# Four cross-attention layers on one core: 32-row score tiles, probabilities transposed on VectorE, weighted sums on 8 or 16 TensorE tiles, five weight matrices reloaded for every batch element

## The chip, the cores and the metric

The kernel runs on one core of one Trainium2 chip. The core has five engines that run side by side and meet at semaphores: TensorE (PE in the profile, with its weight loads as PEld), VectorE (DVE), ScalarE (ACT), GpSimd (POOL) and SyncE (SP, which here only issues DMAs). TensorE reads SBUF and writes PSUM, which has eight banks of 128 partitions x 512 fp32; VectorE and ScalarE read both; GpSimd works on SBUF.

The metric is the device time of one launch in microseconds, lower is better. Everything is fp32.

## The reference

`x` (16 batch elements, 100 queries, width 256) goes through four cross-attention layers against the same context of 361 keys. Layers 0 and 3 have 16 heads of 16, layers 1 and 2 have 16 heads of 64. Cut to what matters:

```python
def attend(Q, K, V, scale):            # per batch element and head
    s = Q @ K.T * scale                # 100 x 361
    return softmax(s) @ V              # 100 x 16 or 100 x 64

# layer 0: layer norms, biases, attention, then a feed-forward block
x = x + attention(ln(x), ln(ctx)) @ wo + bo
x = x + gelu(ln(x) @ w1 + b1) @ w2 + b2          # 256 -> 1024 -> 256
# layer 1: rms norm, heads of 64, no scale
x = x + attention(rms(x), ctx) @ wo              # wq, wk, wv: 256 -> 1024
# layer 2: rotary embedding on q and k, a key mask, norm at the end
x = ln(x + attention(rope(x @ Wq), rope(ctx @ Wk), ctx @ Wv, mask) @ Wo)
# layer 3: as layer 0, without the feed-forward block
x = x + attention(ln(x), ln(ctx)) @ Wo + bo
```

## The kernel before

**A list of works, ordered by a planner.** The Python program first describes the computation as some 560 works for each batch element (`plan.add`): each names the engine or engines that may do it with an assumed occupation and latency, the buffers that it reads and writes, and the buffers that it takes from a pool of slots. `Plan.order` then simulates the engines with these costs, and emits the works in the order that it finds; a copy that may run on ACT or DVE (`copied`, L706) is put on the one that its costs favour. Priorities come from the table `ORDER`: a lag between batch elements, an offset for each place in the list, and further offsets for the first and the last element. All this happens while the kernel is built; on the chip each engine runs a fixed list in order. Two batch elements are in flight, with buffers in two sets by the parity of the element (`kT0`/`kT1` and so on).

**TensorE shapes.** TensorE is used in tiles. A projection runs as four tiles of 128 rows x 32 columns (`on_columns`, L825): one call issues four matmuls, one for each strip of 32 columns of the stationary operand. The planner calls this mode `col32`. Scores run with 32 or 64 rows (`row32`, `row64`), transposes with 64 rows. `Plan.CHANGE` charges a change of mode.

**One attention layer**, class `Attention` (L904): four units of four heads.

1. `scores` (L932, matmul at L936): the stationary operand is a head's queries (100 columns), the moving one its keys, in two halves of 181 and 180. Heads of 16 sit in strips of 32 rows of which 16 are zeroed (`by_parity`, L1202). Each head fills one PSUM bank, 100 partitions x 361; five shares (`ps_sc`) limit how many banks hold scores.
2. `exponential` (L975): DVE takes the scores out of PSUM and finds the row maximum (L991; in layer 2 the mask at L985 and the maximum at L988), ACT does the exponential and its sum (L997).
3. `softmax` (L953): DVE inverts the sums of two heads (L961), POOL multiplies each head by them (L968).
4. `transposed` (L1011): TensorE transposes the probabilities, three chunks of keys by 64 and by 36 queries, 12 transposes for a pair of heads (L1032); ACT or DVE copies them to `pT` (L711, L713).
5. `weighted` (L1052): values are the stationary operand in strips of 32, `pT` the moving one with 100 columns, three chunks of keys (L830); the result is copied to `oT`.

**Around it.** `small_heads_layer` (L1151) and `large_heads_layer` (L1251) make keys (361 columns moving), values (256 or 512 columns moving, keys in chunks of 128, 128 and 105) and queries, and project out (`project_out`, `project_out_T`). `rotated` (L874) does the rotary embedding of layer 2: DVE swaps pairs (L885), POOL multiplies by the sine (L889), DVE multiplies the PSUM original by the cosine (L892), POOL adds (L897). `feed_forward` is L1339, `batch` L1373.

**Weights.** All twelve slabs of 1 MB are loaded once (`load_slab`, L522) through SP's queue in the first 45 us and stay. SP also loads the inputs of element b + 2, each element's mask, and stores its result.

Of the kernel before, what the change touches and what calls it, by code (L numbers as in the profile page):

```python
# [17 lines left out]
P = 128  # L18
# [6 lines left out]
SKP = NKC * KP  # L25
BIG = 3.0e38
SCORE_BANKS = 5
# [4 lines left out]
for _name, _w in (  # L32
# [10 lines left out]

SLABS = (
# [12 lines left out]
    "lag": 281400, "pull": 6.35, "window": 0,  # L57
    "keep": {None: 4180, "row64": 280, "row32": 710, "col64": 3610, "col32": 5250},
    "run": {None: 3260, "row64": 33260, "row32": 18740, "col64": 46890, "col32": 300},
    "batch": (-614500, -19500, 0, 0, 0, 0, 0, 0, 0, 0, 0, 0, 0, 0, 6000, -863500),  # L60
    "place": [
        100 * k for k in (
        1530, 2179, 1302, -155, -3146, -3119, -1447, -50, 2198, -4316, -4647, -2582, -7311,
        -6990, -6791, -975, -6218, -4297, -1712, -7295, -4489, -3822, -7130, -4520, -2986,
        -5107, -1814, 2539, -585, 44, -2295, -3865, -3674, -5144, -5622, -10071, -9468, -6347,
        -6509, -5109, -6468, -10008, -6583, -10112, -6656, -7056, -6274, -9553, -10961, -12648,
        -6592, -6491, -10074, -11842, -5012, -7475, -5864, -2138, -2644, -2757, -1752, -1661,
        -3175, -1806, -475, 295, -1528, -1314, -130, -2596, -3455, -3510, -486, 819, -960, -351,
        -262, -1091, -2095, 773, 352, 609, -2745, -1077, -4127, -3906, 1115, -1980, -1044, 199,
        1113, -2251, -559, -4303, 204, 507, -7028, -6650, -4569, -6483, -2121, -3493, -985,  # L70
        -4030, 928, 291, -3776, -3852, -4367, -2262, -3068, -1405, 3055, -1796, -1471, -2884,
        -3509, -3745, -408, -473, -4075, -5224, -5147, -1610, -3815, -3333, -4064, -6731, -5900,
        -7478, -6211, -2778, -3243, -2860, 346, 2670, -1934, 358, -4143, -3642, -2093, -2165,
        -529, 13, -685, -1077, -415, 5064, -896, -533, -6410, 8, -1286, 795, -1181, 3287, 2325,
        1250, 437, 2327, 2459, -1757, -1578, -5694, -990, 2513, 7808, 7794, 4228, 183, 3326,
        3721, 2104, 3855, 1016, 3932, -5255, -932, -801, -1656, 458, -71, 3547, -2879, -7942,
        1183, -679, -3284, -3147, -4837, -4906, -3658, -1029, -5460, -1795, -2290, -3716, -633,
        -1243, 250, 3042, 115, 3644, 209, 517, 802, 3561, 2033, 8348, 2938, -2370, -768, 91,
        -3053, -3682, 21, -551, -703, 11, -1354, -76, -6811, -5354, -5457, -3261, -4456, -5041,
        -4118, -7857, -5743, -9610, -9289, -7014, -6103, -6155, -5974, -3208, -5827, -5655,  # L80
        -3748, -6019, 1222, -6204, 1169, 1555, 804, 4287, 847, 1540, 2681, 4086, 3349, 8301,
        3405, 2300, 1930, -158, 2379, 3910, 4211, 3253, -272, -266, -2428, -1347, 2024, 88,
        -3112, -7985, -3868, 994, 1277, -1300, -464, -390, 2333, 3472, 2811, 3971, 4406, 6487,
        7550, 8667, 4711, 4737, 1877, 3779, 2319, 8022, 4465, 4476, 4993, 5707, 6778, 4543,
        5848, 4450, 5898, 5280, 5713, 2599, 4430, 8324, 4133, 8528, 6706, 596, 2298, -498, -905,
        1966, -4295, -1105, -3795, -5564, -1315, 1532, -3363, -2789, -552, 18, -3105, -6266,
        -10045, 1320, -6270, -4428, -689, -4740, -3580, 963, -5363, -2314, 1942, 5363, 3756,
        3169, 735, -4085, 2025, 1750, 1971, 2138, 2974, 3519, 5203, 5507, -452, 3042, -190, 412,
        -928, -229, 3162, -526, 895, -1352, -1376, -3942, -3984, -379, -7134, -2812, 551, -6423,
        -2341, -2152, -3333, 1507, -1188, 1764, 4650, 1708, -78, 1087, 3668, 2857, -1320, -858,  # L90
        -553, -1310, -4001, -416, -2796, -2804, -3944, -3808, -3234, -2595, -5780, -8117, -7507,
        -10136, -9612, -9238, -7690, -3249, -4884, -5928, -7611, -6301, -4692, -3495, -11110,
        -9091, -6761, -5493, -6295, -1317, -740, 731, -2244, -69, -536, 1225, -1389, -3686,
        -3052, 1470, -6939, -3363, -3396, -8455, -10700, -13129, -12689, -11245, -7208, -10167,
        -10536, -5830, -7870, -7456, -6041, -4659, -7272, -4839, -3132, -1617, -5559, -2862,
        1514, 625, -188, 1018, -3554, -7159, -3278, -5544, -4708, -2643, -3131, -6058, -6394,
        1652, -6383, 298, -1138, -636, 2469, 408, -1417, 3200, 3186, 3478, 1178, 3587, 3199,
        6766, 4361, -6638, -2795, -3377, -7601, -7151, -544, 106, 696, 3907, 4138, 174, -2346,
        -2919, -5554, -4166, -6125, -7266, -5804, -4121, -1761, -2439, -2442, -6500, -2289,
# [93 lines left out]
        ),  # L193
    },
}

class Buf:
# [209 lines left out]
def tile_xattn_layers(  # L409
# [56 lines left out]
    for t in slots["prob"]:  # L466
        nc.gpsimd.memset(t[:S, SK:], 0.0)
# [1030 lines left out]
```

## Time and profile before

| what | value |
|---|---|
| runs of the kernel before | median 1938.1 us of 3 (1937.89 to 1939.73) |
| the profiled execution, first to last instruction | span 1935.2 us; no other time of this execution is given |
| granted TensorE clock, mean over the span | 0.993 |
| largest TensorE groups, busy: values of the large heads, keys of the large heads, scores, transposes (64 columns) | 367.0, 346.0, 303.3, 240.8 us |
| exponential on ACT, with its read of the sum | 602.0 + 194.0 us in 1024 pairs |
| multiplication by the inverse sum on POOL | 566.2 us in 1024 instructions |
| DMA | 29.94 MB in all, of it 5.64 MB of instructions in 344 packets |

How to read it: a group's busy time is the union of its instructions' durations. TensorE's matmuls are pipelined, so that the durations of neighbours overlap: a matmul with 100 columns has a mean duration of 250 ns, and yet dozens of them start in a microsecond. What TensorE can do in a given time is therefore read from starts, not from durations or from its busy share. The "idle before" of a group is the idle time of its engine just before its instructions, and names who ended it.

### The profile page before, as it was taken

The numbers are of one execution on the slowest core, as the hardware profiler recorded it, in microseconds if no ns is written. First come the engines' busy times: TensorE is split into PE (matmuls) and PEld (weight loads), VectorE is DVE, ScalarE is ACT, GpSimd is POOL, SyncE is SP. The second block draws the span as 40 slices with busy tenths as digits, with TensorE's granted clock in tenths as the row PEclk, the third lists the DMA queues.
The fourth block names the chain that finished last, engine by engine and source line by source line (L and its number), as shares of the span: only waits on it lengthen the run. The fifth ranks groups of instructions, "written<-read, shape, count | busy, mean of one in ns | idle before, by whom it ended". The sixth has DMA issues, their size and how long they took to land.

```text
span 1935.2 us, 99776 instructions
## 1 busy us (share of the span) xinstructions
PE 1914.6 (99%) x43881; PEld 1268.0 (66%) x43881; DVE 1294.5 (67%) x4502; ACT 1170.2 (60%) x3418; POOL 1045.9 (54%) x1682
## 2 busy tenths in 40 slices
PE   8999999999999999999999999999999999999997
PEld 4667666575766757667575675766657576575766
DVE  5556676766667666666666676667676667765776
ACT  4646556575665746657566565665657566575645
POOL 5355465555556555555645555556555555654564
PEclk9999999999999999999999999999999999999997
DMA  7000000000000000000000000000000000000000
GB/s 305 3 3 14 5 12 8 3 14 5 12 8 3 14 5 12 8 3 15 5 14 6 11 9 3 14 5 12 8 3 14 6 12 8 3 15 5 3 3 7
DMA packets 14730, 29.94 MB, mean 15 GB/s; under 512 B 3362, under 2 KB 12376, under 8 KB 12888
## 3 DMA queue, kind: packets, MB, share of 16 engines
q1 hardware_dynamic: 14296, 23.56, 3.8%
q8 instruction: 344, 5.64, 1.2%
q14 instruction: 90, 0.74, 0.1%
HBM read 21.92 MB, written 1.64 MB: 12 GB/s over the span
## 4 chain that ended last, share of the span: by engine, by line
PE 97%; DVE 1%; POOL 1%; ACT 0%; issue 0%; DMA 0%; SPq 0%; POOLq 0%; DVEq 0%; ACTq 0%
PE ps L830 70%; PE ps L936 14%; PE ps L1032 11%; PE ps L771 1%; PE ps L858 1%; PE ps L813 0%; ACT prob L997 0%; DMA slab<-slabs_dram 0%; DVE prob L991 0%; PE ps L616 0%; PE ps L665 0%; POOL prob L968 0%; DVE pT L713 0%; DVE prob L985 0%; POOL kT L897 0%
## 5 line engine op out<-in xcount | busy, mean ns | idle before, releaser
L968 POOL TENSOR_SCALAR prob<-prob,two 100x361 f32<-100x361 f32 x1024 | 566.2, 571 | 551.6 <-DVE two L961 335.2
L997 ACT ACTIVATE prob<-prob,two 100x361 f32<-100x361 f32 x1024 | 602.0, 592 | 138.6 <-DVE prob L991 87.2
L991 DVE TENSOR_SCALAR_CACHE_REDUCE prob<-ps 100x361 f32<-100x361 f32 x768 | 372.3, 530 | 143.7 <-PE ps L936 126.7
L830 PE MATMUL ps<-slab,cT 128*32 128x512 f32 (+1 forms) x3072 | 367.0, 595 | 0.0
L830 PE MATMUL ps<-cT,slab 128*32 128x361 f32 x4096 | 346.0, 468 | 0.0
L936 PE MATMUL ps<-kT,qT 32*100 32x181 f32 (+3 forms) x4096 | 303.3, 328 | 2.9 <-DVE qT L1204 1.4
L711 ACT COPY pT<-ps 128x384 f32<-128x384 f32 (+1 forms) x521 | 231.1, 492 | 93.4 <-PE ps L1032 77.4
L936 PEld LDWEIGHTS ps<-kT,qT 32*100 32x100 f32 (+1 forms) x4096 | 228.1, 164 | 74.8 <-issue 30.8
L1032 PEld LDWEIGHTS ps<-ident,prob 36*128 36x128 f32 (+1 forms) x6144 | 215.3, 140 | 85.1 <-POOL prob L968 62.8
L1032 PE MATMUL ps<-ident,prob 64*128 64x64 f32 (+1 forms) x6144 | 240.8, 227 | 1.5 <-ACT pT L711 0.8
L713 DVE COPY pT<-ps 128x384 f32<-128x384 f32 (+1 forms) x247 | 137.4, 573 | 130.9 <-PE ps L1032 128.7
L711 ACT COPY v<-ps 128x512 f32<-128x512 f32 (+1 forms) x119 | 69.7, 586 | 245.6 <-PE ps L830 161.8
L830 PEld LDWEIGHTS ps<-cT,slab 128*32 128x32 f32 x4096 | 123.1, 109 | 134.7 <-issue 122.4
L997 ACT ACTIVATION_READ_ACCUMULATOR prob<-prob,two 100x1 f32 x1024 | 194.0, 189 | 0.0
L889 POOL TENSOR_TENSOR sw<-sw,rot 128x361 f32<-128x361 f32 x128 | 105.3, 824 | 135.6 <-DVE sw L885 110.2
L830 PEld LDWEIGHTS ps<-slab,cT 128*32 128x32 f32 (+1 forms) x3072 | 85.3, 107 | 139.2 <-issue 127.3
L985 DVE TENSOR_TENSOR prob<-ps,cap 100x361 f32<-100x361 f32 x256 | 125.5, 527 | 62.6 <-PE ps L936 37.9
L830 PE MATMUL ps<-pT,v 128*32 128x100 f32 (+1 forms) x6144 | 155.3, 250 | 0.3 <-ACT pT L711 0.3
L830 PEld LDWEIGHTS ps<-pT,v 128*32 128x32 f32 (+1 forms) x6144 | 136.0, 110 | 22.7 <-issue 13.2
L897 POOL TENSOR_TENSOR kT<-kT,sw 128x361 f32<-128x361 f32 x128 | 122.5, 959 | 5.7
L988 DVE TENSOR_REDUCE two<-prob 100x1 f32<-100x361 f32 x256 | 125.6, 517 | 0.0
L830 PE MATMUL ps<-xT,slab 128*32 128x100 f32 x5120 | 124.1, 252 | 1.1 <-ACT xT L791 1.1
(105 smaller groups left out, 2329.6 us busy)
## 6 DMA issues: line engine op xcount, KB each, us to landing
slab<-slabs_dram SPq DMA_DIRECT2D x11, 1024.0 KB
ctxr<-ctx_dram SPq DMA_DIRECT2D x16, 256.0 KB
ctxr<-ctx_dram SPq DMA_DIRECT2D x16, 105.0 KB
x<-x_dram SPq DMA_DIRECT2D x16, 100.0 KB
out_dram<-x SPq DMA_DIRECT2D x16, 100.0 KB
slab<-slabs_dram SPq DMA_DIRECT2D x2, 512.0 KB
mask<-mask_dram SPq DMA_DIRECT2D x16, 45.1 KB
rows<-rowvecs_dram SPq DMA_DIRECT2D x1, 640.0 KB
```

What stands on the lines that cost most here:

```text
L711: nc.scalar.copy(dst(), src())
L713: nc.vector.tensor_copy(dst(), src())
L830: nc.tensor.matmul(out_f(at + t, at + t1), lhsT=lhsT[:, t:t1], rhs=rhs, start=start, stop=stop, tile_position=(0, at + t),)
L889: nc.gpsimd.tensor_tensor(a, a, wide(sin()), ALU.mult)
L897: nc.gpsimd.tensor_tensor(dst_f(dst.ap), dst_f(dst.ap), sw.ap[:, :n], ALU.add)
L936: nc.tensor.matmul(banks[h].ap[:S, k0:k1], lhsT=self.q_of(h), rhs=self.k_of(h)[:, k0:k1], start=(k0 == 0), stop=(k1 == SK), skip_group_che ...
L968: nc.gpsimd.tensor_scalar(p.ap[:S, :SK], p.ap[:S, :SK], rsum.ap[:S, j : j + 1], 1.0, ALU.mult, ALU.mult,)
L985: nc.vector.tensor_tensor(p(), bank.ap[:S, :SK], self.cap.ap[:S, :], ALU.min)
L988: nc.vector.tensor_reduce(neg_max.ap[:S, 0:1], p(), AX.X, ALU.max, negate=True)
L991: nc.vector.tensor_scalar(p(), bank.ap[:S, :SK], -1.0, None, ALU.mult, ALU.min, accum_out=neg_max.ap[:S, 0:1],)
L997: nc.scalar.activation(p(), p(), AF.Exp, bias=neg_max.ap[:S, 0:1], scale=1.0 if masked else -1.0, accum_out=sums.ap[:S, j : j + 1],)
L1032: nc.tensor.transpose(out[:, c, :], probs[h].ap[q0:q1, c * KP : (c + 1) * KP], ident[q0:q1, q0:q1],)
```

## The change

Every part of attention is cut anew; projections of queries, keys and outputs keep their form.

- **Scores.** The 100 queries are cut into four groups of 25 (`QG`, `QN`). A group's stationary operand is one head's block of 32 columns (25 of the head, 7 of what follows). Four heads lie below each other in the four 32-partition quadrants of one bank, one head per quadrant, and all 361 keys move in one matmul. Heads of 64 run on 8 tiles (64 x 32) and fill 2 banks, heads of 16 on 16 tiles (32 x 32) and fill 4. `qT` becomes flat, with zeros at its end.
- **Softmax.** The same steps on 128 partitions instead of 100; there are as many exponentials, multiplications and PSUM reads as before. Inverse sums come for 2 banks or 4 at once, the masked maximum for 2.
- **Transposes.** One `nc.vector.transpose` of 128 x 768 (blocks of 32 x 32, in place) for each two banks replaces the TensorE transposes and the copies out of PSUM. `pT` holds scores, probabilities and their transposes one after the other; `prob` and the shares are gone.
- **Weighted sums.** Keys come in 12 blocks of 32, the last with 9. One work sums half a layer of large heads (32 x 64 tiles, 8 at a time) or a whole layer of small heads (32 x 32 tiles, 16 at a time) into four banks.
- **Values** are laid out to match: for each block of 32 keys, head pairs go to the quadrants, with 128 (large heads) or 64 (small heads) columns moving instead of 512 or 256.
- **Rotary embedding.** PSUM is copied to `kT` or `qT` by ACT or DVE, and POOL multiplies by the cosine. The bias and parity of the small heads' queries (`by_parity`) may go to ACT too.
- **Weights.** Five slabs are no longer kept; each batch element loads them again into a ring of two slots, through SP, and a load may begin once a named score work has started.
- **Planner.** Modes are named by tile shape; the `ORDER` table is another one.

```diff
-SCORE_BANKS = 5
+NB = 12
+QG = 4
+QN = S // QG
+BLK = 32
+STREAMED = ("L0_xattn_w1", "L0_xattn_w2", "L1_xattn_wo", "L2_xattn_Wq", "L2_xattn_Wo")
...
-        "prob": slots_of("prob", 8, [P, SKP]),
-        "pT": slots_of("pT", 2, [P, 4, NKC, S]),
+        "v": slots_of("v", 3, [P, NB, P]),
+        "ring": slots_of("ring", 2, [P, 2048]),
...
+        slots[f"pT{p}"] = slots_of(f"pT{p}", 2, [P, QG, 2, SKP])
+        slots[f"vs{p}"] = slots_of(f"vs{p}", 1, [P, NB, 144])
+        slots[f"qT{p}"] = slots_of(f"qT{p}", 1, [P, 8 * S + BLK - QN + 1])
...
+    def stream(name, b, begun, after=()):
+        t = plan.buf("ring", f"{name}_{b}")
+        i = SLABS.index((name,))
+        def issue(_):
+            nc.sync.dma_start(out=t.ap, in_=slabs[i])
+        load = plan.add(
+            [("SP", 450.0, 6000.0)], issue, writes=[t], begun=begun
+        )
+        return t, load
...
         def times_cos(_):
-            nc.vector.tensor_tensor(
-                shaped(dst_f(dst.ap)), shaped(ps.ap[:, :n]), wide(cos()), ALU.mult
-            )
+            a = shaped(dst_f(dst.ap))
+            nc.gpsimd.tensor_tensor(a, a, wide(cos()), ALU.mult)
...
-        plan.add(on_dve(n), times_cos, reads=[ps, rot], writes=[dst])
+        copied(lambda: dst_f(dst.ap), lambda: ps.ap[:, :n], n, [ps], [dst])
+        plan.add(on_pool(2.3 * n), times_cos, reads=[dst, rot], writes=[dst])
...
+        def half(self, u, v):
+            name = f"{self.name}_{u}"
+            slots = [plan.buf(f"pT{self.p}", f"{name}_pT{k}") for k in range(self.rows)]
...
+            for g in range(QG):
+                self.group(u, g, slots, parts[g], f"{name}_{g}")
+            self.weighted(u, v, slots, [x for part in parts for x in part], name)
+        def group(self, u, g, slots, parts, name):
...
             def scores(_):
+                for j in range(4):
+                    for t in range(2 * n):
+                        m = 4 * u + j
+                        rows = slice(t * height, (t + 1) * height)
+                        keys = kb[m] if hd == 64 else kb[j // 2]
+                        at = m * S + g * QN
+                        nc.tensor.matmul(
+                            banks[t].ap[j * BLK : (j + 1) * BLK, :SK],
+                            lhsT=q.ap[rows, at : at + BLK], rhs=keys.ap[rows, :],
+                            start=True, stop=True, tile_position=(t * height, j * BLK),
+                        )
...
+                def divide(_, t=t):
+                    a = slots[t // 2].ap[:, g, t % 2, :SK]
+                    nc.gpsimd.tensor_scalar(a, a, inv.ap[:, t : t + 1], 1.0, ALU.mult, ALU.mult)
+                plan.add(on_pool(545), divide, reads=[inv, parts[t]], writes=[parts[t]])
+                if t % 2 == 0:
+                    continue
+                def transpose(_, t=t):
+                    a = slots[t // 2].ap[:, g].rearrange("p r s -> p (r s)")
+                    nc.vector.transpose(a, a)
+                both = parts[t - 1 : t + 1]
+                plan.add(on_dve(2 * SKP), transpose, reads=both, writes=both)
...
+                nc.vector.tensor_reduce(
+                    neg.ap[:, t - 1 : t + 1], slot.ap[:, g, :, :SK], AX.X, ALU.max, negate=True
+                )
...
-        def transposed(self, probs, pairs, name):
...
+        def weighted(self, u, v, slots, parts, name):
...
+            def fn(_):
+                for b in range(NB):
+                    n = keys_in(b)
+                    for j in range(4):
+                        rows = slice(j * BLK, j * BLK + n)
+                        for t in range(P // wide):
...
+                            nc.tensor.matmul(
+                                banks[j].ap[t * wide : (t + 1) * wide, :S].rearrange(
+                                    "p (g s) -> p g s", g=QG
+                                ),
+                                lhsT=lhsT,
+                                rhs=slots[t // 2].ap[rows, :, t % 2, b * BLK : b * BLK + QN],
+                                start=(b == 0), stop=(b == NB - 1),
+                                tile_position=(j * BLK, t * wide),
+                            )
...
-                    for c in range(2):
-                        on_columns(
-                            lambda t0, t1: ps.ap[t0:t1, :], cT.ap[:, c, j * KP : j * KP + n],
-                            w[wv][:, c, half * 512 : (half + 1) * 512], c == 0, c == 1,
-                        )
+                    for k in range(4):
+                        k0 = (4 * i + k) * BLK
+                        for c in range(2):
+                            for j in range(4):
+                                w0 = (4 * u + j) * P
+                                nc.tensor.matmul(
+                                    ps.ap[j * BLK : (j + 1) * BLK, k * P : (k + 1) * P],
+                                    lhsT=cT.ap[:, c, k0 : k0 + BLK], rhs=w[wv][:, c, w0 : w0 + P],
+                                    start=(c == 0), stop=(c == 1), tile_position=(0, j * BLK),
+                                )
...
+        for u in range(2):
+            for m in range(4):
+                keys(4 * u + m)
+            values(u)
+            att.half(u, vb[u])
+        gate = att.first[0, 2]
+        o_buf, _ = stream(wo, b, begun=[gate])
...
+        w1_buf, loaded = stream("L0_xattn_w1", b, begun=[gate])
+        w2_buf, _ = stream("L0_xattn_w2", b, begun=[loaded])
```

## The prediction

> **What bounds the kernel now.** I read the page from its top: busy shares, slices, the chain of work that ended last.
>
> ```profile
> PE 1914.6 (99%) x43881; PEld 1268.0 (66%) x43881; DVE 1294.5 (67%) x4502; ACT 1170.2 (60%) x3418; POOL 1045.9 (54%) x1682
> PE   8999999999999999999999999999999999999997
> PEclk9999999999999999999999999999999999999997
> ...
> PE 97%; DVE 1%; POOL 1%; ACT 0%; issue 0%; DMA 0%; SPq 0%; POOLq 0%; DVEq 0%; ACTq 0%
> PE ps L830 70%; PE ps L936 14%; PE ps L1032 11%; PE ps L771 1%; PE ps L858 1%; PE ps L813 0%; ACT prob L997 0%; DMA slab<-slabs_dram 0%; DVE prob L991 0%; PE ps L616 0%; PE ps L665 0%; POOL prob L968 0%; DVE pT L713 0%; DVE prob L985 0%; POOL kT L897 0%
> ```
>
> TensorE is the end of everything: 97% of the chain. The transposes of the probabilities (L1032) alone are 11% of the span, 213 us. Next the groups that the change touches, then a stretch of the timeline, whose starts give rates.
>
> ```profile
> L968 POOL TENSOR_SCALAR prob<-prob,two 100x361 f32<-100x361 f32 x1024 | 566.2, 571 | 551.6 <-DVE two L961 335.2
> L936 PE MATMUL ps<-kT,qT 32*100 32x181 f32 (+3 forms) x4096 | 303.3, 328 | 2.9 <-DVE qT L1204 1.4
> L711 ACT COPY pT<-ps 128x384 f32<-128x384 f32 (+1 forms) x521 | 231.1, 492 | 93.4 <-PE ps L1032 77.4
> L1032 PEld LDWEIGHTS ps<-ident,prob 36*128 36x128 f32 (+1 forms) x6144 | 215.3, 140 | 85.1 <-POOL prob L968 62.8
> L1032 PE MATMUL ps<-ident,prob 64*128 64x64 f32 (+1 forms) x6144 | 240.8, 227 | 1.5 <-ACT pT L711 0.8
> L713 DVE COPY pT<-ps 128x384 f32<-128x384 f32 (+1 forms) x247 | 137.4, 573 | 130.9 <-PE ps L1032 128.7
> L889 POOL TENSOR_TENSOR sw<-sw,rot 128x361 f32<-128x361 f32 x128 | 105.3, 824 | 135.6 <-DVE sw L885 110.2
> L830 PE MATMUL ps<-pT,v 128*32 128x100 f32 (+1 forms) x6144 | 155.3, 250 | 0.3 <-ACT pT L711 0.3
> L988 DVE TENSOR_REDUCE two<-prob 100x1 f32<-100x361 f32 x256 | 125.6, 517 | 0.0
> ```
>
> ```profile
> 1014.55 1.22 PE L830 MATMUL ps<-pT,v 128*32 128x100 f32 x48
> 1015.70 0.87 PE L936 MATMUL ps<-kT,qT 32*100 32x181 f32 x16
> 1016.50 1.06 PE L830 MATMUL ps<-slab,zT 128*32 128x256 f32 x16
> ...
> 1020.02 0.96 PE L1032 MATMUL ps<-ident,prob 64*128 64x64 f32 x24
> 1020.91 1.92 PE L830 MATMUL ps<-slab,cT 128*32 128x512 f32 x16
> ```
>
> From start to start, 24 transposes take 0.89 us and 16 score matmuls 0.80. The starts of single matmuls say more: on four column tiles they lie 7, 7, 7 ns apart, and a tile starts its next one 86 ns after the last (100 columns), 215 (256), 305 (361) or 430 (512): 2 ns plus 0.833 ns a column. Row tiles keep the same rule (181 columns: 154 ns for four, 152 for two); a pair of transposes takes 61.7. Every fp32 matmul of the code is two in the trace, a transpose one. At these rates all matmuls make 1761 us. Of 948 changes of tile shape, 125 (64-row scores to or from transposes, one shape) cost nothing, the others a median of 90 ns: 74 us. Each of 256 score visits loses about 80 ns on its first weights (20 us), and 12 us pass before the first full stretch. That leaves 68 of the 1935.2: waits, and a tail at half clock:
>
> ```profile
> 0.00:200.00 200.00, 191.22 (x4089) 125.88 (x4089) 116.68 (x421) 112.60 (x320) 97.45 (x179) 0.99 0.21 79
> 200.00:1800.00 1600.00, 1599.42 (x37048) 1054.80 (x37044) 1081.00 (x3763) 982.93 (x2873) 871.66 (x1383) 1.00 0.03 8
> 1800.00:1936.00 136.00, 123.99 (x2756) 87.31 (x2748) 96.81 (x321) 74.66 (x226) 76.79 (x121) 0.90 0.02 5
> ```
>
> (Columns: stretch, its length, busy PE, PEld, DVE, ACT, POOL, clock, DMA.) Before 1800 us TensorE is never short of work, so what leaves it leaves the time.
>
> **TensorE, part by part.**
> Transposes of probabilities: 6144 x 61.7/2 = -189.5 us.
> Scores: large heads 4096 matmuls on 8 tiles make 512 rounds of 303 = 155.1 (now 1024 pairs x 152 = 155.6); small heads 4096 on 16 tiles, 256 rounds = 77.6 (now 78.3). Together -1; first weights of 32 columns in place of 100, 384 visits at some 25 ns: 10 us for 20, -10.
> Weighted sums: large heads 12288 matmuls, 1536 rounds of 86 = 132, as now (6144 x 21.5). Small heads 12288 on 16 tiles: at 6.7 ns a start, sixteen need 107 ns, more than the 86 of the columns, so 768 x 107 = 82 for 66 now: +16 (lower bound 86, +0; upper bound is a rival).
> Values, large heads: 3072 rounds of 128 columns, 108.7 ns = 334 for 329: +5. Small heads: 1536 rounds of 64 columns for 384 of 256 columns (83 us). The trace has no 64-column matmul on four column tiles. By columns 55 ns a round, by the shortest round seen 86: 85 to 132 us. The transposes, 64 columns in 61.7, are the nearest row: 95, +12.
> Changes of shape: 24 score visits, 6 weighted sums and 9 other transposes for each element make 480 changes if most are neighbours and 1248 if none are: 43 to 112 us. I take 60 for each element, about today's 59: 86, +12.
> Instructions: 27,100 matmuls more, each with a weight load. Instruction packets of 16 KB (256 instructions) take 1.08 us and never followed each other within 3.3; a sixteen-tile sum needs three in 2.57. Bounds 0 to 32 x 0.67 = 21; its last packet alone is near the limit: +5.
> Sum -151: -189.5 - 11 + 16 + 17 + 12 + 5.
>
> [...] This trace has 7 ns between tiles. [...]
>
> **The other engines** lose their cover of idle time.
> DVE: -137 (its copies of `pT`), -72 (cosine, 128 x 440 and 32 x 475 ns between starts), -10 (128 inversions fewer at 76), -8 (128 maxima of 722 at 812 for 256 of 361 at 436), and 512 transposes of 768. No row shows one. From L988, 60 + 1.04 ns an element: 860 ns, 440 us, my value, since it too reads and writes SBUF lane by lane; lower bound half (two elements a clock), 205; upper bound two clocks an element, 1660 ns, 850. Sum 1508, of which 190 are copies that ACT may take. [...]
> ACT: 1170 - 231 + about 55 (copies for the rotary embedding) + about 20 (`oT` in 256 pieces of 100, not 128 of 200) = 1015, up to 1180 with DVE's copies.
> POOL: 1046 + 128 x 0.82 + 32 x 1.04 = 1184; 3 us more of memsets at the start, ahead of the first normalization, +0 to 3.
> So at 1805 us DVE stands at 73 to 84%, POOL at 66%, ACT at 56 to 65%: none is the bound. But a weighted sum now waits for 8 or 16 heads instead of 4. On POOL an element's ten cosine products (9 us) stand in the same queue as the multiplications by inverse sums, which DVE's transposes wait for; behind a waiting transpose stand DVE's reads of the other element's scores, and TensorE waits for their banks. The 62.8 us that weight loads idle on POOL at L1032 go to the weighted sums. The waits of 68 become 40 if TensorE meets fewer, 150 if each of DVE's bursts shows; I take 88, as DVE's share rises by a quarter.
> Weights: 80 loads of 1 MB. The stretch from 20 to 40 us moved 389 GB/s, so 2.7 us each, 0.9 us of SP's queue; all bare they cost 216. They are hidden by the rest of a softmax (eight heads keep DVE over 10 us) and by the other element's projections. A load that waits for a ring slot holds SP, and behind it inputs of two elements ahead, the mask and the store: an element (about 110 us) of slack. I take 0, and 0 for the start, where five slabs fewer compete. The query bias's choice of engine, `bq_e` and the flat layouts: 0, hidden under TensorE.
>
> 1935.2 - 150.5 + 20 (waits, 88 for 68) = a span of 1805. The median of the runs lies 2.9 above the profiled span: 1808.
>
> **Rivals.**
> Forecast, 1750 to 1850: TensorE still bounds, 0.50.
> Waits fall, since a TensorE that no longer waits twice for each probability is fed better (for it: 62.8 us of idle; against: busier DVE): waits 40, fewer changes (-40), 64 columns at 55 ns (-10): 1808 - 48 - 40 - 10 = 1710; 1690 to 1750, 0.12.
> Waits grow: DVE's bursts show (layer 2: 16 maskings, 8 maxima, 8 transposes, 10 shuffles, some 28 us, against 18 of TensorE). Waits 150 (+62), changes +26: 1896; 1850 to 1925, 0.14.
> Transposes at two clocks: DVE 1728 to 1918, over 0.97 that is 1782 to 1977, middle 1880; nothing in the trace speaks for it but that fp32 is wide; 0.07.
> Slower: tiles do not overlap beyond four. No matmul of this trace runs beside more than three others. Then the 24,576 weighted matmuls take 21.5 ns each (+314), the 8192 of the scores 76 (+390): 2510. It decides from 4.1 ns lost on each of these 32,768 (134 us). Against it: starts 7 ns apart, and row tiles keep the columns' rule. 0.12.
> No change, by chance of these: 0.03; slower by waits alone (222 us of them instead of 88): 0.02.
>
> A measurement tells some 0.2% (4 us) from no change. Faster: 0.50 + 0.12 + 0.14 + 0.06 of the fourth = 0.82; same 0.03; slower 0.15. Range 1710 to 1910, which leaves out the ends of three cases and the slower one.
>
> **What would show it.** Right: the chain still above 90% TensorE; weighted sums of small heads at about 107 ns for sixteen starts, of large heads 86 for eight; DVE transposes 860 ns apart; weight loads landing before TensorE asks. Wrong: starts of 16 tiles more than 10 ns apart, transposes near 1.7 us, chain shares of DVE above 15%, or TensorE waiting on the ring.

## The result and the profile after

The changed kernel took 2494.7 us, median of 4 runs (2487.5 to 2498.2), beside 1938.0 us of the kernel before in 4 runs on the same chip (1936.0 to 1939.7): 1.287 times as long, 95% interval 1.285 to 1.289. The forecast was 1808. It missed by 687 us and on the wrong side.

The page of the changed kernel, its busy rows, three of the slice and queue rows, the chain by engine, and the groups that the prediction priced:

```profile
span 2489.9 us, 153040 instructions
PE 2082.5 (84%) x71017; PEld 1463.3 (59%) x71017; DVE 1440.8 (58%) x4261; ACT 1098.7 (44%) x3245; POOL 1196.2 (48%) x1840
...
PE   7798878888788888888888988888888888788885
...
PEclk9799998999989998999889998889898999999996
...
q8 instruction: 555, 9.09, 1.5%
...
PE 79%; issue 15%; DVE 3%; POOL 2%; ACT 0%; DMA 0%; SPq 0%; POOLq 0%; DVEq 0%; ACTq 0%
...
L1091 DVE STREAM_TRANSPOSE pT<-pT 128x768 f32<-128x768 f32 x512 | 477.0, 957 | 28.7 <-POOL pT L1083 27.7
...
L1056 PE MATMUL ps<-kT,qT 32*32 32x361 f32 (+1 forms) x8192 | 385.2, 518 | 17.9 <-issue 7.8
...
L1163 PE MATMUL ps<-pT,vs 32*32 32x100 f32 x12288 | 199.6, 296 | 131.0 <-issue 119.5
L1163 PE MATMUL ps<-pT,v 32*64 32x100 f32 x12288 | 196.0, 263 | 102.5 <-issue 98.5
```

What to see: no engine is busy enough to be the bound by its own work. TensorE's share fell from 99% to 84%, VectorE's from 67% to 58%. The chain now has 15% "issue", where before it had 0%: time in which TensorE waited for nothing that the profile shows, no semaphore, no bank, no weights. The weighted sums (L1163) stood idle 234 us, 218 of them on "issue"; the large heads' line before (L830, `pT,v`) 0.3. The packets of instructions went from 344 to 555, as 71,017 matmuls with a weight load each need: 142,034 instructions in 555 packets, 256 to a packet. And the granted clock, at 0.993 before, is 0.914 on the mean: 429 us at half of full speed in place of 31. The packets of the kernel before, by its page:

```profile
q8 instruction: 344, 5.64, 1.2%
```

One such wait, in the chain of the changed kernel (start in us, length in us, what), and under it the DMA row of the same stretch, 1105 to 1121 us in 40 slices of 0.4 us, GB/s; nothing but packets of instructions moves in it:

```profile
1112.72 1.21 PE ps L944 x16
1113.93 2.48 PE ps L1163 x158
1116.41 1.85 issue
1118.26 0.40 PE ps L1163 x8
1118.66 1.35 PE ps L944 x16
```

```profile
GB/s 0 0 0 0 0 41 0 0 0 0 0 0 0 0 0 41 0 0 0 0 0 0 0 0 0 0 0 41 0 0 0 0 0 0 0 41 0 20 0 0
```

A weighted sum starts its matmuls at 13 to 16 ns each, gets through most of its 192 (the trace lacks a few records), and stops for 1.85 us with eight left, the last block of nine keys. A packet begins to arrive at 1115.8 us (the third 41), lands at 1116.7, and some 1.5 us later the sum goes on. The other pauses look the same: there are 265 of over 0.7 us between two starts, the median ends 1.39 us after the landing of a packet, and half of them end 1.32 to 1.48 us after one. Two packets never begin less than 3.25 us apart. A packet holds 128 pairs of weight load and matmul, so that TensorE gets a pair each 25 ns at the closest spacing, and each 27 at 3.5 us, the spacing on the mean in the fastest of the starved streams of experiment 4. A weighted sum uses one in 12 to 16.

Start to start, from the first matmul to the last, TensorE took 1926 us before and 2478.5 after. Of the 552 between them:

| where | us |
|---|---|
| pauses over 0.7 us between starts: 8 with 11 us before, 265 with 465 us after | +454 |
| starts at half clock, by group and shape, mean at half clock less mean at full, times their number: 10 us before, some 120 after | +110 |
| all else, that is, what the forecast's own terms were about (it had -131) | -12 |

### The profile page after: what moved, and what is told of

Its sections match the earlier page's. It is cut to its first block, busy times and chain, and to the rows that moved or that the text cites. A ratio compares the mean times of both kernels' runs of the same rounds, so it can differ in the third digit from the quotient of the medians.

```text
span 2489.9 us, 153040 instructions
## 1 busy us (share of the span) xinstructions
PE 2082.5 (84%) x71017; PEld 1463.3 (59%) x71017; DVE 1440.8 (58%) x4261; ACT 1098.7 (44%) x3245; POOL 1196.2 (48%) x1840
## 4 chain that ended last, share of the span: by engine, by line
PE 79%; issue 15%; DVE 3%; POOL 2%; ACT 0%; DMA 0%; SPq 0%; POOLq 0%; DVEq 0%; ACTq 0%
PE ps L944 29%; PE ps L1163 16%; PE ps L1423 15%; PE ps L1056 14%; PE ps L1336 4%; DVE pT L1112 1%; DVE pT L1091 1%; PE ps L885 1%; PE ps L972 0%; POOL ctxr L861 0%; POOL kT L1007 0%; POOL kT L1010 0%; PE ps L927 0%; POOL sw L1003 0%; POOL mv L850 0%
## 5 line engine op out<-in xcount | busy, mean ns | idle before, releaser
L1083 POOL TENSOR_SCALAR pT<-pT,four 128x361 f32<-128x361 f32 x1024 | 567.3, 576 | 719.7 <-DVE four L1076 718.1
L1136 ACT ACTIVATE pT<-pT,four 128x361 f32<-128x361 f32 x1024 | 601.1, 592 | 190.2 <-DVE pT L1112 115.5
L1091 DVE STREAM_TRANSPOSE pT<-pT 128x768 f32<-128x768 f32 x512 | 477.0, 957 | 28.7 <-POOL pT L1083 27.7
L1112 DVE TENSOR_SCALAR_CACHE_REDUCE pT<-ps 128x361 f32<-128x361 f32 x768 | 364.0, 528 | 159.0 <-PE ps L1056 158.2
L1423 PE MATMUL ps<-slab,cT 128*32 128x128 f32 x12288 | 393.3, 282 | 29.5 <-issue 28.7
L1423 PEld LDWEIGHTS ps<-slab,cT 128*32 128x32 f32 x12288 | 351.7, 114 | 84.3 <-issue 50.1
L1056 PE MATMUL ps<-kT,qT 32*32 32x361 f32 (+1 forms) x8192 | 385.2, 518 | 17.9 <-issue 7.8
L1163 PE MATMUL ps<-pT,vs 32*32 32x100 f32 x12288 | 199.6, 296 | 131.0 <-issue 119.5
L1163 PE MATMUL ps<-pT,v 32*64 32x100 f32 x12288 | 196.0, 263 | 102.5 <-issue 98.5
L1163 PEld LDWEIGHTS ps<-pT,vs 32*32 32x32 f32 x12288 | 159.3, 114 | 172.3 <-issue 141.7
L1163 PEld LDWEIGHTS ps<-pT,v 32*64 32x64 f32 x12288 | 171.3, 135 | 135.3 <-issue 122.3
L1136 ACT ACTIVATION_READ_ACCUMULATOR pT<-pT,four 128x1 f32 x1024 | 195.5, 191 | 0.0
```

What stands on the lines that cost most here:

```text
L1056: nc.tensor.matmul(banks[t].ap[j * BLK : (j + 1) * BLK, :SK], lhsT=q.ap[rows, at : at + BLK], rhs=keys.ap[rows, :], start=True, stop=True, ...
L1083: nc.gpsimd.tensor_scalar(a, a, inv.ap[:, t : t + 1], 1.0, ALU.mult, ALU.mult)
L1091: nc.vector.transpose(a, a)
L1112: nc.vector.tensor_scalar(p(), bank.ap[:, :SK], -1.0, None, ALU.mult, ALU.min, accum_out=neg.ap[:, t : t + 1],)
L1136: nc.scalar.activation(a, a, AF.Exp, bias=neg.ap[:, t : t + 1], scale=1.0 if masked else -1.0, accum_out=sums.ap[:, t : t + 1],)
L1163: nc.tensor.matmul(banks[j].ap[t * wide : (t + 1) * wide, :S].rearrange("p (g s) -> p g s", g=QG), lhsT=lhsT, rhs=slots[t // 2].ap[rows, : ...
```

## The experiments

Two theories were put against each other first. *Supply*: TensorE runs out of instructions, since 128 pairs can't be done in less time than a packet takes to follow the last, 3.25 us at the closest. *Four at a time*: the forecast's rival on the slower side, tiles that don't overlap beyond four. Its price of 2510 us was close to the result, so that it had to be tested. Each of the kernels was timed once, beside the kernel before on the same chip (1936.3 to 1938.0 us). All but the third, the fourth and the tenth start from the changed kernel.

**1. Half the columns, as many instructions.** The weighted sums with 50 columns in place of 100 (the first block keeps all, and the other half is left out):

```diff
+ m = QG if b == 0 else QG // 2
- rhs=slots[t // 2].ap[rows, :, t % 2, b * BLK : b * BLK + QN],
+ rhs=slots[t // 2].ap[rows, :m, t % 2, b * BLK : b * BLK + QN],
```

> The changed kernel, but each matmul of the weighted sums behind the first block of keys moves 50 columns instead of 100 (the sums of the last 50 queries then hold one block of 12). As many instructions, 46% less column work in them. Supply theory (TensorE waits for its instructions, some 3.4 us for each 256 of them): no gain, 2440 to 2500 us. Four-at-a-time theory (tiles beyond four don't overlap, a matmul costs a quarter of its columns' time): 22528 matmuls fall from 21.3 to 10.9 ns, -235, about 2260 us.

2495.9 us. 46% of the columns of 24,576 matmuls taken away, and nothing gained. Its chain, and a group:

```profile
PE 76%; issue 17%; DVE 4%; POOL 2%; ACT 1%; DMA 0%; SPq 0%; POOLq 0%; DVEq 0%; ACTq 0%
...
L1164 PE MATMUL ps<-pT,vs 32*32 32x50 f32 (+1 forms) x12288 | 157.2, 245 | 160.5 <-issue 148.8
```

The group's busy time fell by 42 us, and its idle time on "issue" rose by 29; the clock fell further, to 0.883. The columns don't bind; whatever comes with each instruction does.

**2. Half the instructions, as many columns.** Of each block's weighted matmuls every second one is left out, and the others have 200 columns in place of 100:

```diff
- for t in range(P // wide):
+ for t in range(b % 2, P // wide, 2):
- rhs=slots[t // 2].ap[rows, :, t % 2, b * BLK : b * BLK + QN],
+ rhs=slots[t // 2].ap[rows, :, :, b * BLK : b * BLK + QN],
```

> The changed kernel, but in the weighted sums one matmul moves the 200 columns of two heads and every second one is left out (the sums then mix the heads). Half the instructions there (12288 of 71017 matmuls fewer, each with its weight load), the same columns. Supply theory: taking each 128 pairs of weight load and matmul in program order at the larger of their own time and 3.4 us, the sum falls by 305 us; with a part of the lost clock that is 2050 to 2190 us. Four-at-a-time theory: the same columns cost the same, 2480 to 2500 us.

2108.3 us: 386 less for 12,288 pairs fewer, 31 ns a pair, with the work of the array unchanged. The packets fell to 460 and the pauses over 0.7 us from 465 to 232 us:

```profile
PE 1894.2 (90%) x58729; PEld 1310.5 (62%) x58729; DVE 1434.3 (68%) x4261; ACT 1090.8 (52%) x3245; POOL 1193.2 (57%) x1840
...
q8 instruction: 460, 7.54, 1.5%
...
PE 83%; issue 8%; DVE 5%; POOL 3%; ACT 0%; DMA 0%; SPq 0%; POOLq 0%; DVEq 0%; ACTq 0%
```

**3. The kernel before with more instructions.** Only its weighted sums are changed: each matmul of 100 columns becomes two of 50, on the same four tiles, 9,216 pairs more in all:

```diff
+ for s0 in (0, S // 2):
+     cols = slice(g * S + s0, g * S + s0 + S // 2)
...
- pTs[h][0].ap[:n, pTs[h][1], c, :], c == 0, c == NKC - 1,
+ pTs[h][0].ap[:n, pTs[h][1], c, s0 : s0 + S // 2], c == 0, c == NKC - 1,
```

> The kernel before, but each matmul of its weighted sums is split in two of 50 columns: 9216 pairs of weight load and matmul more, no more columns, the result the same. Supply theory: the sum of the larger of own time and 3.4 us over each 128 pairs rises by 102 us: 2000 to 2080 us. Four-at-a-time theory: nothing here runs on more than four tiles, 1938 to 1950 us.

2026.9 us, 89 more than before, and issue appears in the chain of a kernel that had none:

```profile
PE 95%; issue 3%; DVE 1%; POOL 1%; DMA 0%; ACT 0%; SPq 0%; POOLq 0%; DVEq 0%; ACTq 0%
```

No tile shape, no transpose and no transfer of the change is in this kernel. More instructions for the same columns bring "issue" by themselves: the pauses over 0.7 us went from 11 to 66 us.

**4. Streams by themselves.** Not the kernel: on an otherwise idle core, 2048 pairs of one shape after another, all tiles of the array in turn, with wide matmuls between the streams:

```python
for k in range(count // len(tiles)):
    for r, c in tiles:
        nc.tensor.matmul(
            banks[r // rows][c : c + wide, :n], lhsT=sta[r : r + rows, c : c + wide],
            rhs=mov[r : r + rows, :n], start=True, stop=True, tile_position=(r, c),
        )
```

> No attention, only streams of 1024 fp32 matmul calls (2048 pairs of weight load and matmul) one after the other, each behind 48 calls of 512 columns: four tiles of 128x32 with 100, 64 and 128 columns; eight of 32x64 and sixteen of 32x32 with 100; sixteen of 32x32 with 361; then 512 calls on eight of 64x32 with 361; then twelve times 48 calls on sixteen tiles with 100 columns and 48 calls with 512. Supply theory: 26 to 27 ns a pair in all of the first six, whatever their tiles and columns (128 columns need 27 by themselves), 38 on eight tiles with 361; the short bursts at the end run near 7 ns at their start. Four-at-a-time theory: 21.5, 13.8, 27.2, 21.5, 21.5, 76, 76 ns a pair.

| stream | ns a pair, all 2048 (the last: 1024) | ns a pair, first 128 |
|---|---|---|
| 4 tiles of 128x32, 100 columns | 28.6 | 21.2 |
| 4 tiles of 128x32, 64 columns | 27.5 | 14.1 |
| 4 tiles of 128x32, 128 columns | 28.0 | 27.3 |
| 8 tiles of 32x64, 100 columns | 27.6 | 12.4 |
| 16 tiles of 32x32, 100 columns | 27.1 | 11.2 |
| 16 tiles of 32x32, 361 columns | 28.2 | 23.2 |
| 8 tiles of 64x32, 361 columns | 37.7 | 36.4 |

The chain in the first stream of the table (start, length, what):

```profile
32.97 2.95 PE bank L35 x128
35.92 1.05 issue
36.97 2.95 PE bank L35 x128
39.92 0.78 issue
40.70 2.95 PE bank L35 x128
```

Here the packet can be seen as such: 128 matmuls, a pause, 128 matmuls, a pause, with 3.7 to 4.0 us from one to the next, and nothing else running on the core. Every stream whose first pairs took less than 27 ns ends at 27.1 to 28.6, on 4, 8 and 16 tiles alike; that of 64x32 tiles, with 36.4 in its first pairs, ran without a pause. The first 128 pairs, which lie ready, show what the tiles can do: 8 tiles take 12.4 ns where 4 take 21.2. A limit on how fast TensorE can start pairs would have held these back too. Tiles overlap well beyond four; the rival's mechanism is false, and its 2510 us was a coincidence. Short bursts did no harm: 96 pairs of 16 tiles between matmuls of 512 columns ran at 11.6 ns each on the mean, the first dozen 6 to 7 ns apart, with no pause.

**5. Fewer instructions elsewhere.** The values with 512, or 256 and 128, columns to a matmul, as many columns in all, 13,300 pairs fewer (the values that come out are others):

```diff
- for k in range(4):
-     k0 = (4 * i + k) * BLK
-     ... rhs=w[wv][:, c, w0 : w0 + P],
+ k0, w0 = 4 * i * BLK, 4 * u * P
+ ... rhs=w[wv][:, c, w0 : w0 + 4 * P],
```

> The changed kernel with the values' matmuls made 512, or 256 and 128, columns wide, so that some 13,300 fewer pairs of weight load and matmul are issued; the tiles of the weighted sums and of the scores stay as they are, and the values that come out are not the reference's. Supply theory (no 128 pairs can start faster than one packet of instructions arrives, some 3.4 us): 2250 to 2360 us, from the sum over packets (1974 us of TensorE against 2109 for the changed kernel, and the same 380 us behind it, with some of the stalls in the values' own gone). Rival (TensorE runs at most four tiles of a round at once in the weighted sums): these are untouched, and the values were bound by their columns, so 2470 to 2500 us.

2306.9 us, in the middle of the supply theory's range. The weighted sums, which the edit doesn't touch, gained themselves: 562 us from start to start in place of 616.

**6. Both cuts.** The second and the fifth at once, 45,417 pairs; the scores are untouched.

> Both at once: half of the weighted sums' and scores' smallest matmuls left out as in the second experiment, and the values' wide ones; some 45,000 pairs, about as many as the kernel before has. The sum is left out in part, and the output is not the reference's. Supply theory: 1830 to 1980 us, most likely 1925, with the issue share of the chain under 6%. Rival (four tiles at once): 2470 to 2500 us, since what is left of each round would take as long. A third way: the vector engines become the bound once TensorE is relieved; then the waits of TensorE on VectorE and GpSimd in the chain are above 10% and the time is over 2000.

1959.8 us: 535 of the 557 us are gone. The cuts take 25,600 pairs off, and with them the packets are 356, about as many as before the change. The chain shows who comes next:

```profile
q8 instruction: 356, 5.83, 1.2%
...
PE 78%; DVE 12%; POOL 6%; issue 4%; ACT 0%; POOLq 0%; DVEq 0%; ACTq 0%
```

Issue is at 4%, and VectorE and GpSimd, at 3% and 2% in the changed kernel, are at 12% and 6%. The third way that the expectation named, the vector engines as the next bound, is there by its share of the chain but not by its time.

**7. No reloads.** Two slabs are loaded once and stand for all five weights; the same matmuls in the same order:

```diff
  def stream(name, b, begun, after=()):
-     def issue(_):
-         nc.sync.dma_start(out=t.ap, in_=slabs[i])
...
-     [("SP", 450.0, 6000.0)], issue, writes=[t], begun=begun
+     [("SP", 450.0, 6000.0)], None, writes=[t], begun=begun
```

> The changed kernel with the five weights that are loaded again for each batch not loaded again: two slabs are loaded once and stand for all five, with the same number and order of instructions on TensorE; the values are then those of other weights. Supply theory: the transfers (80 of 1 MB) have no part in it, 2470 to 2510 us. Rival (the reloads delay the packets of instructions, which use the same DMA engines, or TensorE itself): more than 50 us faster, under 2440.

2380.2 us: 114 faster, and the supply theory as I held it, with no part for the transfers, was wrong here. The page has the same work and the same 555 packets:

```profile
PE 2052.6 (86%) x71017; PEld 1448.2 (61%) x71017; DVE 1439.1 (61%) x4261; ACT 1096.7 (46%) x3245; POOL 1196.4 (50%) x1840
...
PE 80%; issue 13%; DVE 4%; POOL 2%; ACT 0%; DMA 0%; SPq 0%; POOLq 0%; DVEq 0%; ACTq 0%
```

In the changed kernel no instruction of TensorE waited for the ring: the weights always landed in time (5.5 us on the median, 7.6 at most, of the 11 loads whose landing the trace tells). What fell is the pauses over 0.7 us, from 465 to 372 us. So the transfers cost nothing by being late themselves; most of what they cost is in longer pauses. Experiments 9 to 11 look at how.

**8. The sums spread out.** Each weighted sum is made into four pieces of three blocks, and TensorE's next works may come between them:

```diff
- def fn(_):
-     for b in range(NB):
+ def fn(_, blocks=range(NB)):
+     for b in blocks:
...
+ pieces[id(made)] = [lambda k=k: fn(None, range(k, k + 3)) for k in range(0, NB, 3)]
...
+ if held and work.engine == "PE":
+     held.pop(0)()
```

> The changed kernel with the weighted sums' matmuls issued in four pieces of three blocks each, with a piece of TensorE's next work between them, and the same matmuls in all. Supply theory: the long stretches of short matmuls are what starves; mixed with wide ones a packet lasts longer, so a gain of up to 200 us less some 50 for more changes of shape: 2300 to 2450 us. It can't fall below some 1930, since 555 packets of 3.47 us are still needed. Rival (tiles not overlapping): the same matmuls take as long wherever they stand, and the changes of shape come on top: 2490 to 2560 us.

2477.9 us, 17 less than the median of the changed kernel's runs, which lie 11 us apart: little, and outside both expectations. But the sums were hardly spread. What is left of a sum is issued at once when the next work of any engine uses one of its buffers, and in the trace most of the 32 sums of the small heads still run their 384 matmuls in one piece, and most of the 64 of the large heads are broken once, into 48 and 144. So the run does not show what spreading would bring. The supply theory's range was a guess; worked out afterwards for the order that ran, it gives none of that gain. Taking TensorE's time for each 128 pairs in their order, by the rates of the prediction, and never less than 3.36 us, an estimate from the packets' spacing (3.25 at the closest), the sum is 2094 us for the changed kernel and 2091 for this one: 368 and 369 of 555 packets are below the limit either way. Most neighbours of a weighted sum are values and projections, whose pairs need 14 to 28 ns: they have nothing to spare. And at 27.1 ns a pair, the fastest that a stream of the fourth experiment kept up, 71,017 pairs would take 1925 us in any order, about the time of the kernel before.

**9. Both cuts and no reloads.** The sixth and the seventh together.

> The sixth experiment (half of the smallest matmuls left out, wide values; 1959.8 us) without the five weights' reloads, as in the seventh, which took 114 us off the changed kernel. It computes the values of other weights and leaves out part of the sums. If the reloads cost by delaying packets of instructions, they cost less where TensorE seldom runs out of instructions: 1910 to 1945 us. If they cost in another way, about as much as in the changed kernel whatever TensorE runs: 1840 to 1860 us.

1924.7 us: without reloads 35 us less, not 114. Where TensorE seldom runs dry, the same transfers cost a third. That fits transfers that delay packets, and the expectation for them (1910 to 1945). The time is 0.6% under the kernel before, with part of the sums left out, so it is no candidate. It says something else: with 355 packets and nothing to load, it is still not near 1808. Its chain:

```profile
PE 77%; DVE 12%; POOL 6%; issue 3%; DMA 1%; ACT 1%; SPq 0%; POOLq 0%; DVEq 0%; ACTq 0%
```

**10. Streams beside transfers.** The 16-tile stream of 100 columns, 2048 pairs, three times alone and three times after eight 1 MB transfers were started, and then twelve pauses of 2.9 us before wide matmuls.

> Not the kernel, but streams alone: 1024 pairs of weight load and matmul on 16 tiles of 32x32, 100 columns, three times without and three times with 1 MB transfers in flight on the sync queue, and then 12 pauses of some 2.5 us (TensorE waits for VectorE copies) with 48 matmuls of 512 columns after each. If transfers delay the packets: 128 pairs behind a packet take 4 to 4.6 us with the transfers and 3.4 to 3.6 without. If not, 3.4 to 3.6 in both. For the clock: if any pause of 2.5 us lowers the granted clock, the 512-column matmuls after the pauses run at half of it; if only something in the stretches of short matmuls does, they stay at the full clock.

Alone 56.0, 57.5 and 54.8 us, with the transfers 64.9, 64.6 and 63.3. In the windows (stretch, its length, busy PE and PEld, DVE, POOL, clock, DMA share, GB/s): a stream alone, the beginning of one beside transfers, its end, and the pauses. Then the chain in the second of them:

```profile
18.00:72.00 54.00, 35.79 (x1981) 27.99 (x1969) 4.08 (x4) 0.00 (x0) 0.55 0.02 5
88.00:108.00 20.00, 7.82 (x438) 6.06 (x425) 0.00 (x0) 0.00 (x0) 0.58 0.98 410
108.00:150.00 42.00, 27.09 (x1439) 21.02 (x1440) 0.00 (x0) 0.00 (x0) 0.50 0.02 6
460.00:620.00 160.00, 127.10 (x1128) 35.61 (x1120) 30.41 (x44) 0.00 (x0) 0.97 0.00 1
```

```profile
93.21 3.94 issue
97.15 2.44 PE bank L35 x117
99.58 3.76 issue
103.34 2.44 PE bank L35 x113
105.78 3.76 issue
109.54 2.44 PE bank L35 x118
111.98 1.02 issue
```

While the DMA engines are 98% busy, packets begin 5.9 to 6.8 us apart, and the pauses are 3.8 us; when the transfers end, the pause is 1.0 again and the packets 3.3 to 4.0 us apart. So transfers in flight add some 2.6 us to a packet that is wanted just then: 128 pairs take longer than the 4 to 4.6 us expected for this case, and far longer than the 3.4 to 3.6 expected if transfers do nothing. TensorE itself is not slowed: the 113 to 118 matmuls between two pauses take 2.44 us here and in the fourth experiment. Each of the kernel's 80 reloads cost 114/80 = 1.4 us.

The clock, the column before the last two, is the second result. After most pauses of 2.9 us the wide matmuls keep it, 0.97; two of the twelve were followed by half clock, for 6.8 and 3.4 us. In the stream of 32x32 tiles it is about a half even alone (0.55), where the pauses are some 1 us. The windows of the fourth experiment have three starved streams and stretches of wide matmuls: two of 128-row tiles with 100 and 64 columns, which kept 1.00, and then the stream of 32x32 tiles with 100 columns:

```profile
60.00:120.00 60.00, 42.52 (x1920) 35.57 (x1920) 0.00 (x0) 0.00 (x0) 1.00 0.02 4
120.00:180.00 60.00, 49.53 (x1836) 42.34 (x1839) 0.00 (x0) 0.00 (x0) 1.00 0.02 4
300.00:360.00 60.00, 45.40 (x1758) 27.73 (x1739) 0.00 (x0) 0.00 (x0) 0.61 0.02 4
```

The stream of 32x64 tiles was at half clock for 17 of its 57 us, and that of 32x32 tiles with 361 columns kept full clock. So pauses of this length did not lower it by themselves: the streams of 128-row tiles had them too. What lowers it, these runs do not show.

**11. Smaller transfers.** Each reload as four issues of 512 columns:

```diff
- nc.sync.dma_start(out=t.ap, in_=slabs[i])
+ for k in range(4):
+     part = slice(k * 512, (k + 1) * 512)
+     nc.sync.dma_start(out=t.ap[:, part], in_=slabs[i][:, part])
```

> The changed kernel with each reload of 1 MB issued as four transfers of 512 columns (2 KB a row in place of 8). If a packet of instructions stands behind the transfer's large pieces on the DMA engines, smaller pieces let it through sooner: 2390 to 2460 us. If it is the number of bytes in flight that delays it, no change: 2480 to 2510 us; if each issue on the queue costs the packets something, slower: over 2510.

2484.9 us, 2.6 below the lowest of the changed kernel's four runs, and as expected if the bytes count: rows of 2 KB in place of 8 did not let the packets through sooner.

## Why the prediction was wrong

**The step that failed is "Instructions".** It had both numbers: 27,100 matmuls more, and packets that "never followed each other within 3.3" us. It then asked only whether one weighted sum could outrun its packets, allowed 0.67 us for each of the 32 sixteen-tile sums of the kernel as the upper bound, 21 us, and took 5. The 0.67 is what three transfers of 1.08 us take beyond the sum's 2.57; at the spacing of 3.3 that the same sentence names, three packets take 9.9. The runs put some 535 us on the number of instructions, with the clock and the delays that hang on it (experiment 6). Three things were wrong with the step. It took packets as an accident of single bursts, where they are a rate: 71,000 pairs are 555 packets, and 555 times 3.3 is 1830 us. That alone, two numbers from the trace and one multiplication, stands above the 1808 that I forecast (at the closest spacing of the changed kernel, 3.25, it would be 1804; at the 27.1 ns a pair that a stream kept up, 1925). It looked at the weighted sums only; the values with 64 columns (14.5 ns a pair) and the projections with 100 (some 22) also need less than 27 ns, and the values with 128 (27.6) hardly more, so little refilled what a sum had drained. And it left out that the kernel before was near the limit in places already, which 9,216 more pairs showed (experiment 3). "Before 1800 us TensorE is never short of work, so what leaves it leaves the time" held for the kernel before; its converse was not asked: what comes to TensorE in instructions comes to the time.

**Weights, taken at 0.** Half right: they landed before TensorE asked, and nothing waited on the ring. But the cover was named only for the weights. The transfers' other effect, on the packets of instructions, cost 114 us in this kernel and 35 in one with slack (experiments 7, 9, 10); the upper bound in the text, 216 all bare, held by luck, as it was meant for another cost. Some 65 to 80 of the 111 us between the two traces, by how a transfer's time is counted, lie in pieces of 64 matmuls with a transfer under way; where the rest comes from is not settled.

**The clock** was no term at all: some 110 us more than before by the trace, which has half clock for 429 us in place of 31, in 59 stretches, 58 of them one to four times 3.41 us long. What sets a stretch off was not shown: the stream of experiment 10 has half clock (0.50 to 0.58 on the mean of its windows) while short matmuls of 32 rows keep the array running, with pauses of some 1 us, and two of that experiment's twelve pauses of 2.9 us were followed by it.

**Weighted sums.** The forecast had 6.7 ns a start on 16 tiles (107 ns for sixteen) and 86 ns for eight starts. At full clock and outside the pauses they come at 11.8 and 13.0 ns: +63 and +28 us. The prediction's own mark for wrong, "starts of 16 tiles more than 10 ns apart", was met, but only as a mis-sized term: the stream by itself has 11.2 and 12.4.

**Scores.** On 8 tiles of 64 rows, 36.6 ns a start for the 37.9 forecast: right. On 16 tiles of 32 rows, 38.6 for 18.9: +80 us. Part of it is waiting: the weight loads of these scores stood idle 63 us until VectorE had read earlier scores (L1112). The first packet of the stream, without such waits, has 23.2, so the 18.9 was too low as well.

**Values.** 128 columns 27.6 ns for 27.2 and 64 columns 14.5 for 15.5, outside the pauses: right, and of no use, as TensorE did not keep getting pairs faster than one in 27.

**Removed work and changes of shape.** The transposes' 189.5 us did leave. Changes of shape were forecast between 480 and 1248, with 960 taken. Counted as there, with rows and columns rounded up to 32, 64 or 128 (the kernel before then has 823 that cost something), there are 516. The 86 us were taken from too many changes.

**The other engines.** VectorE's transposes take 882 ns (median, from the start of one to the start of the next instruction with no idle time between) for the 860 forecast; VectorE is at 1441 us for 1508, GpSimd at 1196 for 1184, ScalarE at 1099 for 1015 to 1180: right, and none binds in the changed kernel. Whether they would have at 1805 us is another matter: experiment 9 has less work on TensorE than the forecast, little starvation and no reload, and stands at 1925 with 18% of its chain on VectorE and GpSimd. So the waits taken at 88 seem to have been too few as well, by an amount that these runs don't separate from the sums' rates. No run shows the working lane by lane that the transposes' 860 ns were argued from, nor the elements a clock behind its bounds of 205 and 850 us; what the runs show is 957 ns a transpose on the mean, 477 us in all.

**The rivals.** The slower side was priced 2510 for tiles that don't overlap beyond four. Experiments 1 and 4 refute it. What the prediction set against it, starts 7 ns apart, holds for a burst on 16 tiles too: there starts lie 6 to 7 ns apart, and a stream has 11.2 ns over its first 128 pairs. Over a long stretch it does not hold: the supply made 27 to 28.6 ns for a pair with its weight load. Going by the 7 ns was right for the overlap of the tiles and wrong for the sum: a rate seen over four starts says nothing of what can be kept up.

No version that beats both kernels came out. Those that were fast left out work; with 71,000 pairs there is hardly room below the time of the kernel before, 1925 us at 27.1 ns a pair. Forms of the change with fewer and wider matmuls for the same result were not tried.

## What to carry to other kernels

Count instructions as a resource with its own rate. From the page's instruction queue take the packets and how close they ever came; packets after the change times that spacing is an estimate of the least that the engine needs for the whole kernel; a short burst that lies ready can run faster (96 pairs at 11.6 ns each). Here the spacing was 3.25 us at the closest and 3.5 to 3.7 on the mean in the starved streams, so where TensorE is the bound, a weight load with its matmul was worth replacing by two smaller ones only while each kept the array busy for more than 27 ns. "issue" in the chain of a TensorE that is not busy, with pauses that end much the same time after a packet's landing (half of them 1.32 to 1.48 us here), is how this looks afterwards; and a transfer that is never waited for can still cost, through the packets that it delays (80 transfers of 1 MB cost 114 us here).

## What the runs showed of the hardware

- The spacing of packets of instructions is 3.25 us at the least in the changed kernel (3.22 in all runs) and 3.5 to 3.7 on the mean in the starved streams, though a packet's own transfer takes 1.07 us; with the DMA engines 98% busy it is about 6 us.
- No stream kept up weight load and matmul faster than one pair in 27 ns, on 4, 8 or 16 tiles; the first 128 pairs of the shortest ran at 11 to 14 ns.
- The granted clock fell to half in streams of 32x32 tiles with 100 columns at 27 ns a pair, stayed at 1.00 in starved streams of 128-row tiles, and at 0.97 over pauses of 2.9 us between wide matmuls.
